# Layer 0 of a two-layer transformer: softmax division traced one step later, block transposes held in place on VectorE, two tails advanced together

## The chip, the core and the metric

The kernel runs on one core of a Trainium2 chip. A core has five engines that run side by side, each through its own list of instructions in order: TensorE (PE, matrix products; PEld is its loading of weights), VectorE (DVE), ScalarE (ACT), GpSimd (POOL) and SyncE (SP, which here only issues DMA transfers). They wait for one another through semaphores. The metric is the time of one execution in microseconds of device time, the median of several runs; lower is better.

## The reference, cut to what matters

The input `x` is 4 sequences of 256 tokens with 512 numbers each, in float32. Two layers follow, each an attention block and a feed-forward block, each with a residual sum and a layer norm after it:

```python
x = L0_attn_x
x = _layernorm(x + _L0_attn_ref(x, ...), axis=-1)
x = _layernorm(x + _L0_ffn_ref(x, ...), axis=-1)
x = _layernorm(x + _L1_attn_ref(x, ...), axis=-1)
x = _layernorm(x + _L1_ffn_ref(x, ...), axis=-1)
```

The change concerns the attention of layer 0: 32 query heads of 16 numbers, 8 key and value heads (each shared by 4 query heads), and a causal mask over 256 tokens:

```python
scores = jnp.einsum('bhqd,bhkd->bhqk', q, k) / jnp.sqrt(jnp.asarray(HEAD_DIM, dtype=jnp.float32))
scores = jnp.where(causal, scores, NEG)
p = jax.nn.softmax(scores, axis=-1)
out = jnp.einsum('bhqk,bhkd->bhqd', p, v)
out = out.transpose(0, 2, 1, 3).reshape(B, S, D_MODEL)
return out @ Wo + bo
```

Its feed-forward block is one product with a 512 x 512 weight, dequantised in the kernel, and a bias. Layer 1's attention has 32 query heads of 128 numbers and a distance bias.

## The kernel before

The kernel is written with a framework that traces instructions in program order, then orders each engine's list by priorities and a plan of its own, and adds the semaphores. Where the code calls `tc.keep_in_program_order(ins)`, the instruction keeps its place in program order on its engine; all others may be moved. Buffers come from pools; a tile with `bufs=n` has n places that are used in turn, and a new tile waits until the old user of its place is done.

**Layer 0's steps.** The work is 64 steps `(b, qt, h, i)`: sequence `b` (4), query tile `qt` of 128 tokens (2), half `h` of the heads (2), and `i` (4). A step handles 4 query heads for 128 queries against 128 keys (`qt` 0) or 256 keys (`qt` 1). It passes through these stages:

- `begin0`: two score products on TensorE (L470) into one of two PSUM tiles `sc`; VectorE adds the causal mask (L475) and takes the negated row maxima `nm` (L478); ScalarE computes four exponentials into `pr` with their row sums `sums` (L274, one instruction and a read of the accumulator each); then `divided`: VectorE's reciprocal of the sums (L279) and GpSimd's multiplication of `pr` by it (L280).
- `transpose0`: the probabilities have to be transposed before the output product. There are two ways. TensorE transposes four 128 x 128 blocks into PSUM (L295) and ScalarE copies them to `prT` (L296, or L102/L100 for the first tiles). Or `transposed_by_blocks`: VectorE transposes 32 x 32 blocks within `pr` (L306), SP stores the result to device memory in four pieces (`way<-blocks`, L312) and loads it back in the right order (`prT<-way`, L316).
- `end0`: after the last `i` of a half, the output products (L515) into `o`; after both halves a copy of `o` to `oT` (L100 on VectorE or L102 on ScalarE in turn), and a tail for this tile of 128 tokens is queued.

`run` drives the steps: at count n it begins step n, calls `fill`, transposes step n - `lag`, and ends step n - `lag` - `more`. Before, both are 3.

**Between the steps.** `fill` advances two queues by one piece each. `ahead` holds `project0(b + 1)`: the transposes of `x` and the key, query and value products of the next sequence (L270, L376, L389, L404). `tails` holds `feed_forward_weight` first and then the tails, `tail0`: output projection (L428), residual sum (L430), layer-norm statistics (L257 to L259), a power on GpSimd (L260), normalisation (L264), transposes of the result `x1` (L270), the addition of the feed-forward bias on GpSimd (L440), the feed-forward product (L444), sum, statistics, power and normalisation again (L448, L257 to L260, L264), and the transposes of the result into `x2T` (L270). A tail is cut into pieces by `yield`; an empty piece (a second `yield` in a row) is a pause. Only the tail at the head of the queue advances.

**The way into layer 1.** The last tails run beside the first products of layer 1: at L717 seven pieces of `project1(0)` alternate with pieces of the tails. Sums over the tokens of `x2T` on GpSimd (`token_sums`, L589 to L592) come after the third. Layer 1 itself (from L682) also uses `divided` and `transposed_by_blocks`, the latter with `room` 2 where layer 0 has 1.

Of the kernel before, what the change touches and what calls it, by code (L numbers as in the profile page):

```python
# [21 lines left out]
B, S, D = 4, 256, 512  # L22
# [37 lines left out]
def block_kernel(  # L60
# [20 lines left out]
    nc = tc.nc  # L81
# [52 lines left out]
    def bank_m(name):  # L134
        return ps_w.tile([P, D], F32, tag="w", name=name)
# [116 lines left out]
    def norm_factors(y, name):  # L252

        st = s0.tile([P, 6], F32, tag="bn", name=f"bn_{name}", bufs=4)
        mv = s0.tile([P, 2], F32, tag="mv", name=f"mv_{name}", bufs=4)
        rs = s0.tile([P, 1], F32, tag="rs", name=f"rs_{name}", bufs=4)
        nc.vector.bn_stats(st, y)  # L257
        nc.vector.bn_aggr(mv, st)
        nc.vector.tensor_scalar(rs, mv[:, 1:2], EPS, 1.0, ALU.add, ALU.mult)  # L259
        powers.append(nc.gpsimd.tensor_tensor(rs, rs, minus_half, ALU.pow))  # L260
        return mv[:, 0:1], rs

    def normalise(dst, y, factors):
        nc.vector.tensor_scalar(dst, y, *factors, ALU.subtract, ALU.mult)  # L264

    def transposed(dst, src, name):

        pt = bank_t(f"pt_{name}")
        for c in range(NC):
            nc.tensor.transpose(pt[:, c, :], src[:, ts(c, P)], ident)  # L270
        evacuate(dst, pt)

    def exponentials(pr, sc, nm, sums, i, w):
        nc.scalar.activation(  # L274
            pr[:, i, 0:w], sc, AF.Exp, bias=nm[:, i : i + 1], accum_out=sums[:, i : i + 1]
        )

    def divided(pr, sums, w):
        nc.vector.reciprocal(sums, sums)  # L279
        nc.gpsimd.tensor_tensor(  # L280
            pr[:, :, 0:w], pr[:, :, 0:w], sums.unsqueeze(2).to_broadcast([P, G, w]), ALU.mult
        )

    def softmax_tiles(sp, name, bufs):
        nm = sp.tile([P, G], F32, tag="nm", name=f"nm_{name}", bufs=bufs + 2)
        sums = sp.tile([P, G], F32, tag="sums", name=f"sums_{name}", bufs=bufs + 2)
        pr = sp.tile([P, G, 2 * P], F32, tag="pr", name=f"pr_{name}", bufs=bufs)
        return nm, sums, pr
# [9 lines left out]
    def transposed_by_blocks(sp, name, pr, nt, dst, room):  # L298

        blocks = sp.tile(
            [P, room, 4, G, 32], F32, tag="blocks", name=f"blocks_{name}", bufs=2 // room
        )
        for kt in range(nt):
            nc.vector.transpose(  # L306
                blocks[:, kt].rearrange("p j h q -> p h j q"),
                pr[:, :, ts(kt, P)].rearrange("p h (j k) -> p h j k", k=32),
            )
        way = dram.tile([2, 4, 32, 4, G * 32], F32, tag="way", name=f"way_{name}")  # L310
        for i in range(4):
            nc.sync.dma_start(  # L312
                way[0:nt, :, :, i, :].rearrange("t j k f -> k (t j) f"),
                blocks[32 * i : 32 * i + 32, 0:nt].rearrange("k t j h q -> k (t j) (h q)"),
            )
        nc.sync.dma_start(  # L316
            dst.rearrange("p t j h q -> p t (j h q)"),
            way[0:nt].rearrange("t j k i f -> (j k) t (i f)"),
        )

    def run(steps, begin, transpose, end, before, fill, lag, more=1, after=None):

        waiting = deque()
        for n in range(len(steps) + lag + more):
            if n < len(steps):
                before(steps[n])
                waiting.append([steps[n], begin(*steps[n])])
            fill()
            if lag <= n < len(steps) + lag:
                item = waiting[min(n - lag, more)]  # L330
                item[1] = transpose(*item[0], item[1])
            if n >= lag + more:
                step, got = waiting.popleft()
                end(*step, got)
            if after:
                after()

    def advance(queue):

        while queue:  # L340
            if next(queue[0], None) is not None:
                return
            queue.popleft()

    def exhaust(queue):
        while queue:
            advance(queue)


    qkv0 = {}  # L350
# [73 lines left out]
    def tail0(tt, oT):  # L424

        py = bank_m(f"py_{tt}")
        for i in range(G):
            nc.tensor.matmul(py, oT[:, i, :], wop[:, i, :], start=(i == 0), stop=(i == G - 1))  # L428
        y = s0.tile([P, D], F32, tag="y", name=f"y_{tt}")
        nc.vector.tensor_tensor(y, py, x[tt], ALU.add)  # L430
        factors = norm_factors(y, f"a{tt}")
        yield True
        x1 = s0.tile([P, D], F32, tag="x1", name=f"x1_{tt}")
        normalise(x1, y, factors)
        yield True
        if tt < NTT - 1:
            yield True
        x1T = s0.tile([P, NC, P], F32, tag="x1T", name=f"x1T_{tt}")
        transposed(x1T, x1, f"x1_{tt}")
        nc.gpsimd.tensor_tensor(x1, x1, fb_b, ALU.add)  # L440
        yield True
        pf = bank_m(f"pf_{tt}")
        for c in range(NC):
            nc.tensor.matmul(  # L444
                pf, x1T[:, c, :], wfT[:, c, :], start=(c == 0), stop=(c == NC - 1)
            )
        y2 = s0.tile([P, D], F32, tag="y", name=f"y2_{tt}")
        nc.vector.tensor_tensor(y2, pf, x1, ALU.add)  # L448
        factors = norm_factors(y2, f"b{tt}")
        yield True  # L450
        x2[tt] = xp.tile([P, D], F32, tag="x", name=f"x2_{tt}")
        normalise(x2[tt], y2, factors)
        yield True
        if tt < NTT - 1:
            yield True
        transposed(x2T[:, :, ts(tt, P)], x2[tt], f"x2_{tt}")
        yield True

    ahead, tails = deque(), deque()

    def begin0(b, qt, h, i):

        qT, kT, _ = qkv0[b]
        w = (qt + 1) * P
        name = f"0_{b}_{qt}_{h}_{i}"
        nm, sums, pr = softmax_tiles(a0, name, 6)
        sc = ps_s0.tile([P, 2, 2, 2 * P], F32, tag="s", name=f"sc_{name}")
        for j in range(2):
            rows = slice(32 * (2 * h + j), 32 * (2 * h + j) + 32)
            nc.tensor.matmul(  # L470
                sc[:, j, :, 0:w], qT[rows, i, ts(qt, P)], kT[rows, :, 0:w], start=True, stop=True
            )
        scf = sc.rearrange("p j e k -> p (j e) k")
        diag = scf[:, :, w - P : w]
        nc.vector.tensor_tensor(  # L475
            diag, diag, causal.unsqueeze(1).to_broadcast([P, G, P]), ALU.add
        )
        nc.vector.tensor_reduce(nm, scf[:, :, 0:w], AX.X, ALU.max, negate=True)  # L478
        for n in range(G):
            exponentials(pr, scf[:, n, 0:w], nm, sums, n, w)  # L480
        divided(pr, sums, w)
        return pr

    open0 = {}
    def transpose0(b, qt, h, i, pr):


        name = f"0_{b}_{qt}_{h}_{i}"
        if i == 0:
            open0["p", h] = a0.tile(  # L490
                [P, 2, G, 4, 4, 32], F32, tag="prT", name=f"prT0_{b}_{qt}_{h}"
            )
        prT = open0["p", h]
        rest = range(qt + 1)
        if (0, 0) < (b, qt) and (b, qt, h) < (B - 1, 1, 1) and (qt == 1 or i % 2 == 0):
            rest = rest[1:]
            transposed_by_blocks(a0, name, pr, 1, prT[:, 0:1, i], 1)
        copy = evacuate if (b, qt) == (0, 0) else nc.scalar.copy
        transposed_probabilities(
            name, pr, [(kt, prT[:, kt, i].rearrange("p j n q -> p n j q")) for kt in rest], copy  # L500
        )
        return prT
# [35 lines left out]
                load_weights1(0)  # L538

    def fill():  # L540
        advance(tails)
        advance(ahead)

    ahead.append(project0(0))
# [6 lines left out]
        before0,  # L551
        fill,
        lag=3,
        more=3,
    )
    la.close()

# [158 lines left out]

    first = project1(0)  # L717
    for n in range(7):
        advance(tails)
        if n == 2:  # L720
            with tc.issue_after(powers[-1].ins):
                token_sums(0, 3 * P)
        next(first)
# [105 lines left out]
    kept = [m1.tile([P, 2, 2, 2 * P], F32, name=f"kept_{b}") for b in range(B)]  # L829
# [199 lines left out]
        for _ in range(due - 1):  # L1029
            advance(ahead)  # L1030

    def after1(newest_first=False):

        for tail in list(tails)[:: -1 if newest_first else 1]:
            if next(tail, None) is None:
                tails.remove(tail)

    run(
        [(kv, b, qt) for kv in range(NKV) for b in range(B) for qt in range(2)],
        begin1,  # L1040
# [2 lines left out]
        before1,  # L1043
        fill1,
        lag=1,
        after=after1,
    )
    while outputs or tails:
        advance(outputs)
        ending.append(True)  # L1050
        after1(True)


# [30 lines left out]
```

## Time and profile before

| | |
|---|---|
| time, median of 3 runs (lowest to highest) | 994.2 us (992.19 to 995.15) |
| the profiled execution's own time | 993.61 us |
| its span | 991.4 us |
| instructions in its profile | 11477 |
| mean granted TensorE clock over the span | 0.975 |
| layer 0 (until the first product of layer 1 starts) | 0 to 303 us |
| layer 1 and the end | 303 to 991.4 us |
| VectorE's block transposes in layer 0 (L306, 25 to 303 us) | 40, of 0.71 us |

One execution was recorded by the hardware profiler. "Busy" is the time in which an engine ran instructions; TensorE's products overlap and their ends are modelled, so a busy TensorE need not be one at its peak. The granted clock is the share of full speed that TensorE was allowed. The view of waits says for which instruction an engine with nothing to do was waiting; the chain of waits follows the work back from the last instruction to whatever released each step. L numbers are lines of the kernel before. Records of a few products are missing from a trace.

### The profile page before, as it was taken

The numbers are of one execution on the slowest core, as the hardware profiler recorded it, in microseconds if no ns is written. First come the engines' busy times: TensorE is split into PE (matmuls) and PEld (weight loads), VectorE is DVE, ScalarE is ACT, GpSimd is POOL, SyncE is SP. The second block draws the span as 40 slices with busy tenths as digits, with TensorE's granted clock in tenths as the row PEclk, the third lists the DMA queues.
The fourth block names the chain that finished last, engine by engine and source line by source line (L and its number), as shares of the span: only waits on it lengthen the run. The fifth ranks groups of instructions, "written<-read, shape, count | busy, mean of one in ns | idle before, by whom it ended". The sixth has DMA issues, their size and how long they took to land.

```text
span 991.4 us, 11477 instructions
## 1 busy us (share of the span) xinstructions
PE 941.6 (95%) x3433; PEld 546.3 (55%) x3433; DVE 620.6 (63%) x1287; ACT 316.3 (32%) x1198; POOL 443.2 (45%) x461
## 2 busy tenths in 40 slices
PE   7989979989989999999999999999999999999996
PEld 5634444443334444566666666666666666667652
DVE  3757766656754345755566666667666666666566
ACT  2545544445451100332312222222222121223442
POOL 2344443443444611443633534543544453467732
PEclk9889999989899999999999999999999999999998
DMA  9325234234322010344443353434353334243001
GB/s 286 127 75 128 67 91 108 63 86 108 75 54 85 21 43 0 75 138 115 123 113 117 113 145 86 145 87 126 97 141 103 107 92 132 76 127 88 1 21 63
DMA packets 105218, 95.42 MB, mean 96 GB/s; under 512 B 9157, under 2 KB 76358, under 8 KB 105158
## 3 DMA queue, kind: packets, MB, share of 16 engines
q1 hardware_dynamic: 104342, 93.26, 33.9%
q10 hardware_dynamic: 816, 1.44, 0.4%
q8 instruction: 27, 0.44, 0.2%
q14 instruction: 33, 0.27, 0.1%
HBM read 60.07 MB, written 34.60 MB: 95 GB/s over the span
## 4 chain that ended last, share of the span: by engine, by line
PE 74%; POOL 11%; DVE 7%; ACT 3%; issue 2%; DMA 2%; SPq 0%; POOLq 0%; DVEq 0%; ACTq 0%
PE p_q L615 18%; PE po L858 14%; PE sc L945 7%; PE o L985 7%; POOL pr L280 5%; PE p_k L615 5%; PE p_v L615 5%; PE o L515 3%; ACT pr L274 3%; PE py L819 3%; PE sc L470 3%; DVE nm L478 2%; PE pt L295 2%; DVE blocks L306 2%; PE pq L389 2%
## 5 line engine op out<-in xcount | busy, mean ns | idle before, releaser
L274 ACT ACTIVATE pr<-sc,nm 128x256 f32<-128x256 f32 (+1 forms) x512 | 208.8, 419 | 408.1 <-DVE nm L961 284.3
L280 POOL TENSOR_TENSOR pr<-pr,sums 128x512 f32<-128x512 f32 (+1 forms) x128 | 188.1, 1470 | 286.6 <-DVE sums L279 270.9
L306 DVE STREAM_TRANSPOSE blocks<-pr 128x512 f32<-128x512 f32 x124 | 85.9, 702 | 76.5 <-POOL pr L280 75.5
L953 DVE SCALAR_TENSOR_TENSOR sc<-table,sc 128x128 f32<-128x128 f32 (+1 forms) x256 | 86.0, 356 | 34.7 <-PE sc L945 32.4
L274 ACT ACTIVATION_READ_ACCUMULATOR pr<-sc,nm 128x1 f32 x512 | 103.7, 203 | 0.0
L945 PEld LDWEIGHTS sc<-kT,qT 128*128 128x128 f32 x512 | 82.3, 191 | 35.2 <-issue 29.2
L945 PE MATMUL sc<-kT,qT 128*128 128x256 f32 (+1 forms) x512 | 95.2, 327 | 0.0
L985 PE MATMUL o<-prT,v 128*128 128x512 f32 x192 | 92.9, 593 | 0.0
L629 DVE TENSOR_TENSOR qT<-p_q,qT 128x512 f32<-128x512 f32 x96 | 64.6, 686 | 35.6 <-PE p_q L615 34.8
L470 PE MATMUL sc<-kT,qT 32*128 32x256 f32 (+1 forms) x256 | 62.8, 568 | 16.7 <-ACT pr L274 16.6
L961 DVE TENSOR_REDUCE nm<-sc 128x2 f32<-128x512 f32 (+1 forms) x128 | 70.2, 551 | 1.5
L478 DVE TENSOR_REDUCE nm<-sc 128x4 f32<-128x512 f32 (+1 forms) x64 | 60.8, 950 | 1.0
L858 PE MATMUL po<-wo,so 128*128 128x256 f32 x224 | 58.0, 381 | 2.1 <-POOL so L595 2.1
L615 PE MATMUL p_q<-x2T,ws_q 128*128 128x512 f32 x128 | 59.8, 592 | 0.0
L615 PE MATMUL p_q<-xt,ws_q 128*128 128x512 f32 x128 | 57.8, 593 | 1.8 <-POOL ws_q L598 1.8
L858 PE MATMUL po<-wo,o 128*128 128x256 f32 x224 | 57.7, 380 | 0.0
L615 PE MATMUL p_q<-x2T,wq 128*128 128x512 f32 x128 | 57.6, 592 | 0.0
L515 PE MATMUL o<-prT,v 128*32 128x512 f32 x192 | 55.8, 670 | 1.0 <-DMA prT<-way 0.7
L102 ACT COPY o<-o 128x512 f32<-128x512 f32 x29 | 17.0, 585 | 124.6 <-PE o L985 124.6
L858 PE MATMUL po<-to,so 128*128 128x256 f32 x224 | 53.3, 381 | 1.0 <-POOL so L598 1.0
L279 DVE RECIPROCAL sums<-sums 128x4 f32<-128x4 f32 x128 | 21.9, 171 | 50.1 <-ACT pr L274 49.8
L858 PEld LDWEIGHTS po<-to,so 128*128 128x128 f32 x224 | 42.2, 190 | 16.3 <-issue 8.8
(156 smaller groups left out, 1430.3 us busy)
## 6 DMA issues: line engine op xcount, KB each, us to landing
way<-blocks SPq DMA_DIRECT2D x272, 64.0 KB, 1.8
prT<-way SPq DMA_DIRECT2D x68, 256.0 KB, 2.7
way<-blocks SPq DMA_DIRECT2D x112, 128.0 KB, 2.5
prT<-way SPq DMA_DIRECT2D x28, 512.0 KB, 3.7
wq<-in_L_attn_w_qkv_dram SPq DMA_DIRECT2D x8, 1024.0 KB, 5.1
wo<-in_L_attn_w_o_dram SPq DMA_DIRECT2D x8, 1024.0 KB, 5.1
wk<-in_L_attn_w_qkv_dram SPq DMA_DIRECT2D x4, 512.0 KB, 3.7
wv<-in_L_attn_w_qkv_dram SPq DMA_DIRECT2D x2, 1024.0 KB, 6.2
```

The lines of the kernel that those rows point to most:

```text
L274: nc.scalar.activation(pr[:, i, 0:w], sc, AF.Exp, bias=nm[:, i : i + 1], accum_out=sums[:, i : i + 1])
L280: nc.gpsimd.tensor_tensor(pr[:, :, 0:w], pr[:, :, 0:w], sums.unsqueeze(2).to_broadcast([P, G, w]), ALU.mult)
L306: nc.vector.transpose(blocks[:, kt].rearrange("p j h q -> p h j q"), pr[:, :, ts(kt, P)].rearrange("p h (j k) -> p h j k", k=32),)
L470: nc.tensor.matmul(sc[:, j, :, 0:w], qT[rows, i, ts(qt, P)], kT[rows, :, 0:w], start=True, stop=True)
L478: nc.vector.tensor_reduce(nm, scf[:, :, 0:w], AX.X, ALU.max, negate=True)
L515: nc.tensor.matmul(o[32 * r : 32 * r + 32, :], v[:, kt, r, ts(e, 32)], prT[:, kt, :, :, 2 * j + e, :], start=(kt == 0 and e == 0), stop=(k ...
L615: nc.tensor.matmul(bank, fixed, moving, start=(c == 0), stop=(c == 1))
L858: nc.tensor.matmul(bank[:, ts(n, HALF)], left[:, c, :], right[:, c, :], start=(c == 0), stop=(c == 1),)
L945: nc.tensor.matmul(sc[:, m, 0:w], qT[:, 2 * j + m, b * S + qt * P : b * S + (qt + 1) * P], kT[:, b * S : b * S + w], start=True, stop=True,)
L953: nc.vector.scalar_tensor_tensor(sc[:, m, 0:w], table[:, 2 * P - w :], slopes[kv * G + 2 * j + m], sc[:, m, 0:w], ALU.mult, ALU.add,)
L961: nc.vector.tensor_reduce(nm[:, 2 * j : 2 * j + 2], sc[:, :, 0:w], AX.X, ALU.max, negate=True)
L985: nc.tensor.matmul(o, v1[:, 2 * b + kt, ts(kv, P)], prT[:, kt].rearrange("p j h q -> p h j q"), start=(kt == 0), stop=(kt == qt),)
```

## The change

It has five parts, all in layer 0.

- The division of a step is no longer traced in its own `begin0`. The step's `pr` and `sums` go into `undivided`, and `divide0` divides them in the next step's `begin0`, after that step's exponentials are traced (or in `rest` when there is no next step). The reciprocal keeps its place in program order.
- The block transposes of layer 0 (`room` 1) keep their place in program order on VectorE.
- For `qt` 1 the first three of four `i` go through block transposes where all four did; the fourth goes through TensorE. For `qt` 0 it stays with `i` 0 and 2.
- `fill` advances every tail in the queue by one piece (`advance_all`) where it advanced the first one; two pauses are added to each tail but the last. In layer 1 `advance_all` takes the place of `after1`, which did the same.
- `more` goes from 3 to 2: a step ends, and the output products are traced, one step earlier.

```diff
-    def divided(pr, sums, w):
-        nc.vector.reciprocal(sums, sums)
+    def divided(pr, sums, w, kept=False):
+        ins = nc.vector.reciprocal(sums, sums)
+        if kept:
+            tc.keep_in_program_order(ins)
         nc.gpsimd.tensor_tensor(
...
-            nc.vector.transpose(
+            ins = nc.vector.transpose(
                 blocks[:, kt].rearrange("p j h q -> p h j q"),
                 pr[:, :, ts(kt, P)].rearrange("p h (j k) -> p h j k", k=32),
             )
+            if room == 1:
+                tc.keep_in_program_order(ins)
...
-    def run(steps, begin, transpose, end, before, fill, lag, more=1, after=None):
+    def run(steps, begin, transpose, end, before, fill, lag, more=1, after=None, rest=None):
...
                 waiting.append([steps[n], begin(*steps[n])])
+            elif rest:
+                rest()
             fill()
...
+    def advance_all(queue, newest_first=False):
+
+        for work in list(queue)[:: -1 if newest_first else 1]:
+            if next(work, None) is None:
+                queue.remove(work)
...
         if tt < NTT - 1:
             yield True
+            yield True
         x1T = s0.tile([P, NC, P], F32, tag="x1T", name=f"x1T_{tt}")
...
         if tt < NTT - 1:
+            yield True
             yield True
         transposed(x2T[:, :, ts(tt, P)], x2[tt], f"x2_{tt}")
...
-        divided(pr, sums, w)
+        divide0()
+        undivided.append((pr, sums, w))
         return pr
 
     open0 = {}
+    undivided = []
+
+    def divide0():
+
+
+        if undivided:
+            divided(*undivided.pop(), True)
+
...
-        if (0, 0) < (b, qt) and (b, qt, h) < (B - 1, 1, 1) and (qt == 1 or i % 2 == 0):
+        if (0, 0) < (b, qt) and (b, qt, h) < (B - 1, 1, 1) and i in ((0, 2), (0, 1, 2))[qt]:
             rest = rest[1:]
             transposed_by_blocks(a0, name, pr, 1, prT[:, 0:1, i], 1)
...
     def fill():
-        advance(tails)
+        advance_all(tails)
         advance(ahead)
...
         lag=3,
-        more=3,
+        more=2,
+        rest=divide0,
     )
...
     for n in range(7):
-        advance(tails)
+        advance_all(tails)
```

More of the change, by code (lines that the diff above doesn't have):

```diff
@@ L1030, in fill1 @@
             advance(ahead)
[L1032 to L1036, printed above, removed]
     run(
@@ L1045, in block_kernel @@
         lag=1,
-        after=after1,
+        after=lambda: advance_all(tails),
     )
@@ L1050, in block_kernel @@
         ending.append(True)
-        after1(True)
+        advance_all(tails, True)
 _INS = [
```

## The prediction

> **What bounds the kernel now.** I read the page first, then the stretches of time, then who waited for whom, then one piece of the chain of waits. On the page (rows 1 and 2) TensorE is busy 95% of the span, but the second row shows where it is not: its digits fall below 9, and the granted clock below full, in the first 13 of 40 slices, which is layer 0 (slice 40 is the end of the program).
>
> ```profile
> PE 941.6 (95%) x3433; PEld 546.3 (55%) x3433; DVE 620.6 (63%) x1287; ACT 316.3 (32%) x1198; POOL 443.2 (45%) x461
> ...
> PE   7989979989989999999999999999999999999996
> ...
> PEclk9889999989899999999999999999999999999998
> ```
>
> The table of stretches (length, busy us of PE, PEld, DVE, ACT, POOL, then granted clock and DMA share) splits layer 0 by sequence:
>
> ```profile
> 76.00:151.00 75.00, 67.18 (x292) 34.66 (x292) 52.89 (x103) 38.63 (x154) 34.32 (x29) 0.94 0.38 98
> 151.00:226.00 75.00, 67.64 (x278) 32.16 (x277) 49.01 (x94) 35.58 (x144) 31.92 (x26) 0.91 0.35 86
> 25.00:303.00 278.00, 250.12 (x1040) 120.21 (x1039) 181.59 (x343) 140.17 (x557) 118.11 (x93) 0.92 0.34 87
> ```
>
> From 25 to 303 us TensorE idles 278.0 - 250.1 = 27.9 us, and its clock averages 0.92, which is 0.08 x 278 = 22 us of full-speed time not granted. No other engine is near full (DVE 65%, ACT 50%, POOL 42%, DMA 34%), so the stalls are waits. The waits in the same stretch (total us, times, longest):
>
> ```profile
> PE sc L470 <- ACT pr L274: 16.6, 12, 3.8
> PE pt_x L270 <- DVE x L264: 4.7, 3, 1.7
> ```
> ```profile
> ACT pr L274 <- DVE nm L478: 70.2, 31, 6.2
> ```
> ```profile
> DVE blocks L306 <- POOL pr L280: 30.0, 24, 2.1
> DVE sums L279 <- ACT pr L274: 21.0, 19, 3.7
> ```
>
> TensorE waits for a score bank that ScalarE's exponentials still hold, ScalarE waits for VectorE's maxima, and VectorE stands 51 us, with later maxima queued behind it, for a block transpose whose probabilities GpSimd has not divided, or for sums not yet added up. The chain of waits (start, us, what) has it in one piece:
>
> ```profile
> 49.59 1.90 POOL pr L280
> ...
> 51.52 0.71 DVE blocks L306
> ...
> 52.46 1.90 POOL pr L280
> ...
> 54.39 0.71 DVE blocks L306
> 55.10 0.60 DVE sc L475
> ...
> 59.05 2.08 PE sc L470 x4
> ```
>
> Two divisions, each followed by its own block transpose, put the mask at 55.1; TensorE idles from 56.0 to 59.05.
>
> [...]32.34 to 35.75 us eight matmuls of L376 take 3.41 us where the same eight take 1.92 later, and the clock is 0.50 in 30-35 us and in 205-210 us, each after a stall. [...]
>
> **The change, part by part.** Its order of instructions on each engine, beside that of before, gives the counts.
>
> *Division a step later.* Of the 63 reciprocals of layer 0 that have a next step, before has 25 ahead of the next mask, 14 between mask and maxima, 24 after the maxima; now all 63 come after. The wait of a reciprocal for ScalarE (21.0 us) therefore stands behind maxima already handed over. Eight exponentials take 1.94 us (row of 47.21 us in the chain), mask and maxima 0.68 + 1.22 = 1.90 us, so little wait is left. Queued behind it now: block transposes and copies, and GpSimd's multiply (1.90 us), which has idle time.
>
> *Block transposes pinned.* Before, 20 of 40 follow their own reciprocal with no mask or maxima between; now 31 of 33 come two or three maxima after it, some 8 us, against 1.90 us of multiply. The 30.0 us wait goes from VectorE. Late next is the tail: an output product, its sum, statistics, a power on GpSimd, the normalisation, all ahead of a mask. At 121-130 us this holds the maxima for 8.7 us and TensorE for 3.8; I expect about 1.3 of the 3.8 to stay, since only one 0.71 us transpose and some of the waiting leave that piece.
>
> *Seven transposes to TensorE.* Block transposes fall from 40 to 33: 7 x 0.71 = 5.0 us off VectorE, and 35 DMA issues off SP (28 stores, 7 loads). Neither is on the path: VectorE will have slack and DMA is at 34%. TensorE gets 7 x 4 transposes. Four take 0.60 to 0.66 us in the trace; with a weight load and the switch ahead of them 0.76 more in the worst rows. I take 0.9 each: **+6.3 us**, bounds 7 x 0.6 = 4.2 and 7 x 1.42 = 10. All of it lies on the path, TensorE being the bound. ScalarE gets 7 copies of 0.60 us = 4.2, covered by its 50% idle time; without that cover they would delay exponentials by the same 4.2 us.
>
> *Tails two at once, a pause longer.* No instruction more. On GpSimd's queue a tail's power (0.55 us) now goes ahead of a multiply (1.90 us) that it used to follow, in most tails of sequences 1 to 3. The transposes of x1 and x2 stand later in TensorE's order, after the power and normalisation they wait for (the 4.7 us row, and 1.5 us of L295 behind the same). At the end of layer 0 the x2 transposes of tile 6 move past the first key product (3.43 us); the sums over tokens on GpSimd, which began at 306.71 behind a power, then start about 1.2 us later, covered by the output product before 317. I add **+0.5**, bounds 0 to 3.
>
> *One step less before the output product.* Nothing added or removed; see the slower rival.
>
> *Gain in stalls:* 75% of 16.6 = 12.5; of 4.7 + 1.5, 80% = 5; of 2.2 us of transposes waiting for a division, 0.7 (the last at 284 us stays). Sum **-18**. *Gain in clock:* 22 us were lost; [...]I take half of it, rounded down: **-10**. Bounds on both: only 8 and 3, if the tails set the maxima; 24 and 20, if hardly a stall is left.
>
> Layer 1's instructions and their order are unchanged; it only starts earlier. Sum: -18 - 10 + 6.3 + 0.5 = -21.2. The profiled execution took 993.6 (span 991.4 and 2.2 around it), 0.6 below the median of 994.2; taken off it gives 972.4, and I centre on the median: **973**. The mechanism's ends are 994 - 44 + 4 = 954 and 994 - 11 + 10 = 993.
>
> **The rivals.** *The clock stays low (983).* [...]For it: at 146.6-149.5 two gaps of 0.7 and 1.5 us were enough for 0.52 afterwards. Against: 100-125 us has gaps of 0.4 to 1.8 and a clock of 1.00. Then -18 + 6.8 = -11.
>
> *The change does little of what it says (990).* The order already had 24 reciprocals behind the maxima, and VectorE's next wait (8.4 us for output products at L100, 8.1 for scores at L475) takes the place of the removed ones. Then -8 - 3 + 6.8 = -4.
>
> *Slower: the transposed blocks come too late (1011).* Their way through memory is 0.71 us of transpose, four stores of 0.43 us to issue, 1.8 us to land, a load of 2.8 us: about 7 us. On SP a load is queued behind the first stores of the next block, which wait for that block's pinned transpose. Before, 4 to 5 steps lay between the last transpose of a half and the product at L515; now about 3, some 12 us, so 5 us are left at the tightest place. If steps shorten to 2.3 us, or the queue adds 5, the product waits. Behind it wait the copy of `o`, and in three places VectorE's maxima, which now stand after that copy. At 2 us in each of 14 halves, and no clock gained: -21 + 28 + 10 = +17. Against it: only 1.7 us of waiting for these loads before, and fewer DMAs.
>
> **How the numbers follow.** A measurement of this kernel tells about 0.3% (3 us) from no change. The main case has 0.62, the low clock 0.16, the small effect 0.10, the slow case 0.12. The first two are faster by over 3 us, and half of the small effect: 0.83; the other half, 0.05, is no change; 0.12 slower. The range of 957 to 993 leaves out the slow case and the far ends of the main one.
>
> **What would show it.** Right: the waits of L306 for GpSimd and of L279 for ScalarE fall from 51 to under 12 us; TensorE's wait for the exponentials under 6; the start of layer 1's first product (303 us) near 282; granted clock over layer 0 about 0.96. The added transposes show as 251 instead of 223 instructions of L295 in that stretch. Wrong: L515 waiting for its load over 5 us in all, VectorE's copy of `o` growing well past 8.4 us with maxima behind it, or the first product of layer 1 after 300.

## The result, and the profile after

The changed kernel takes **982.4 us** (median; 981.7 to 983.7), the kernel before 993.2 (four executions; the table above has three of them). The ratio is 0.989, 95% interval 0.987 to 0.991: about 11 us faster, half of the 21 forecast, inside the range of 957 to 993.

The page of the changed kernel (span 981.8 us; the busy row, then 40 slices of the span):

```profile
PE 936.3 (95%) x3461; PEld 546.8 (56%) x3461; DVE 615.1 (63%) x1280; ACT 320.7 (33%) x1205; POOL 444.8 (45%) x461
...
PE   7999999979889999999999999999999999999996
...
PEclk9999999997899999999999999999999999999999
```

The first nine slices now have a clock of 9 tenths or more; before, it fell to 8 in slices 2, 3, 9 and 11. But TensorE is busy 7, 9, 8 and 8 tenths in slices 9 to 12, with a clock of 7 and 8 tenths in slices 10 and 11: that is sequence 3 (202 to 271 us) and the end of layer 0; a slice is 24.5 us. The table of stretches, cut at the first maxima of sequences 1, 2 and 3, at the last maxima and at layer 1's first product (columns as in the prediction, the last column GB/s), of the changed kernel and then of the kernel before:

```profile
25.00:69.19 44.19, 42.00 (x226) 25.31 (x224) 37.93 (x72) 29.08 (x114) 24.37 (x18) 1.00 0.34 107
69.19:134.62 65.43, 61.70 (x280) 31.57 (x280) 47.88 (x90) 36.88 (x148) 31.42 (x26) 1.00 0.32 81
134.62:202.23 67.61, 63.70 (x280) 31.79 (x280) 47.88 (x91) 36.85 (x147) 31.38 (x26) 0.97 0.32 79
202.23:271.39 69.16, 59.24 (x208) 23.49 (x208) 40.49 (x77) 34.09 (x140) 26.01 (x22) 0.83 0.29 72
271.39:293.09 21.70, 17.91 (x76) 7.75 (x77) 4.35 (x9) 7.17 (x21) 6.63 (x5) 1.00 0.05 16
```
```profile
25.00:81.44 56.44, 49.30 (x221) 29.22 (x221) 39.70 (x74) 29.35 (x115) 25.37 (x19) 0.85 0.34 104
81.44:152.42 70.98, 64.01 (x276) 31.88 (x273) 48.89 (x93) 35.15 (x143) 31.23 (x26) 0.96 0.37 94
152.42:226.71 74.29, 66.93 (x275) 31.96 (x273) 48.30 (x92) 35.58 (x146) 31.05 (x25) 0.91 0.34 86
226.71:284.22 57.51, 52.87 (x206) 20.11 (x203) 40.35 (x79) 34.84 (x144) 25.35 (x21) 0.93 0.38 93
284.22:302.95 18.73, 16.96 (x70) 6.97 (x69) 4.36 (x8) 5.25 (x15) 5.11 (x4) 1.00 0.00 1
```

So by the start of sequence 3 the change has won 12.25 + 5.55 + 6.68 = **24.5 us**, more than the forecast for the whole; sequence 3 and the end then **give back 14.6**. TensorE's busy column splits both: up to sequence 3 it idles 21.5 us before and 9.8 after, and is busy 12.8 us less with no product fewer, so at a higher clock (0.99 against 0.91 over this part); from there on it idles 7.3 us more and is busy 7.3 us more, at a lower one (0.87 against 0.95). Layer 1 takes 688.7 us (688.5 before).

The waits from 25 to 293 us (total, times, longest), TensorE's and VectorE's:

```profile
PE sc L484 <- ACT pr L274: 8.1, 6, 3.3
PE pt L297 <- POOL pr L282: 7.2, 5, 2.0
PE o L538 <- DMA prT<-way: 3.3, 2, 1.8
...
DVE sc L489 <- PE sc L484: 26.5, 18, 3.6
DVE y L442 <- PE py L440: 16.2, 7, 6.9
DVE y L461 <- PE pf L457: 15.8, 7, 8.9
DVE oT L100 <- PE o L538: 15.4, 5, 4.9
DVE sums L279 <- ACT pr L274: 6.1, 6, 2.4
```

The 51 us that VectorE stood for sums and multiplies have become 6.1. It now waits for TensorE's products instead, once for 6.9 us, and its idle time as a whole has only gone from 96.4 (278.0 - 181.6) to 89.6 us (268.1 - 178.5). On TensorE the wait for exponentials has halved (16.6 before), and the wait for probabilities that GpSimd has not yet divided has grown from 2.2 to 7.2. The timeline of TensorE and VectorE shows the place of the 6.9 us (start, us; in brackets the idle time before it and what ended it):

```profile
255.48 1.13 PE L484 MATMUL sc<-kT,qT 32*128 32x512 f32 x4 [1.92 <-ACT pr L274]
...
257.79 2.07 PE L484 MATMUL sc<-kT,qT 32*128 32x512 f32 x2 [1.18 <-ACT pr L274]
...
259.79 5.78 PE L440 MATMUL py<-wop,oT 128*128 128x512 f32 x8
...
265.61 0.69 DVE L442 TENSOR_TENSOR y<-py,x 128x512 f32<-128x512 f32 x1 [6.91 <-PE py L440]
```

Two score products meet with nothing between them, and each waits for the exponentials. The clock drops (0.50 from 259 to 262 us). The second product is cut in two by the scheduler, and its other half (at 265.94) stands behind an output projection that takes 5.78 us at the low clock (3.70 at 225 us, at a clock of 1.00). VectorE stands for the projection's result, whose sum is ahead of the mask in its queue: 11.7 us pass without new maxima.

### The profile page after: what moved, and what is told of

It reads as the page before. It is cut to its first block, busy times and chain, and to the rows that moved or that the text cites. A ratio compares the mean times of both kernels' runs of the same rounds, so it can differ in the third digit from the quotient of the medians.

```text
span 981.8 us, 11455 instructions
## 1 busy us (share of the span) xinstructions
PE 936.3 (95%) x3461; PEld 546.8 (56%) x3461; DVE 615.1 (63%) x1280; ACT 320.7 (33%) x1205; POOL 444.8 (45%) x461
## 4 chain that ended last, share of the span: by engine, by line
PE 82%; POOL 7%; DVE 5%; ACT 2%; DMA 1%; issue 1%; SPq 0%; POOLq 0%; DVEq 0%; ACTq 0%
PE p_q L639 18%; PE po L882 14%; PE sc L969 8%; PE o L1009 8%; PE p_k L639 5%; PE p_v L639 5%; PE o L538 5%; PE sc L484 4%; PE pf L457 3%; PE py L440 3%; PE py L843 3%; PE pq L401 3%; PE pt L297 2%; POOL pr L282 2%; ACT pr L274 2%
## 5 line engine op out<-in xcount | busy, mean ns | idle before, releaser
L308 DVE STREAM_TRANSPOSE blocks<-pr 128x512 f32<-128x512 f32 x117 | 80.5, 697 | 45.8 <-POOL pr L282 45.5
L484 PE MATMUL sc<-kT,qT 32*128 32x256 f32 (+1 forms) x256 | 66.1, 561 | 8.3 <-ACT pr L274 8.1
L985 DVE TENSOR_REDUCE nm<-sc 128x2 f32<-128x512 f32 (+1 forms) x128 | 70.1, 550 | 1.5
L489 DVE TENSOR_TENSOR sc<-sc,causal 128x512 f32<-128x512 f32 x64 | 43.9, 686 | 29.2 <-PE sc L484 29.0
L297 PE MATMUL pt<-ident,pr 128*128 128x128 f32 x300 | 45.3, 279 | 11.3 <-POOL pr L282 9.2
L297 PEld LDWEIGHTS pt<-ident,pr 128*128 128x128 f32 x300 | 34.2, 141 | 34.5 <-issue 16.8
```

Of the source, the lines that this page charges most:

```text
L297: nc.tensor.transpose(pt[:, i, :], pr[:, i, ts(kt, P)], ident)
L308: ins = nc.vector.transpose(blocks[:, kt].rearrange("p j h q -> p h j q"), pr[:, :, ts(kt, P)].rearrange("p h (j k) -> p h j k", k=32),)
L484: nc.tensor.matmul(sc[:, j, :, 0:w], qT[rows, i, ts(qt, P)], kT[rows, :, 0:w], start=True, stop=True)
L985: nc.vector.tensor_reduce(nm[:, 2 * j : 2 * j + 2], sc[:, :, 0:w], AX.X, ALU.max, negate=True)
```

## The experiments

Each kernel is one of the two with a change that is shown further down. The stretches are those above, from the profiled run (sequence 0 from 25 us on); "end" is the last one. The ratio is to the kernel before on the same chip. A row of stretches is one execution, and the executions of one kernel can differ by several us (u_seven 993.8 to 1005.0, d_div_pin 993.6 to 1001.5), so a difference of 2 or 3 us in one stretch is not shown to repeat.

| kernel | us | ratio [95%] | seq. 0 | seq. 1 | seq. 2 | seq. 3 | end |
|---|---|---|---|---|---|---|---|
| before | 993.2 | 1 | 56.4 | 71.0 | 74.3 | 57.5 | 18.7 |
| after | 982.4 | 0.989 [0.987, 0.991] | 44.2 | 65.4 | 67.6 | 69.2 | 21.7 |
| u_div | 996.1 | 1.004 [1.002, 1.006] | 50.9 | 69.6 | 65.2 | 70.1 | 24.6 |
| u_pin | 985.1 | 0.991 [0.989, 0.994] | 48.7 | 68.7 | 68.3 | 59.9 | 21.0 |
| u_seven | 997.6 | 1.006 [1.004, 1.007] | 43.6 | 73.9 | 73.1 | 65.1 | 23.0 |
| u_tails | 981.1 | 0.989 [0.985, 0.992] | 43.9 | 67.4 | 68.0 | 67.3 | 18.6 |
| u_i123 | 994.5 | 1.001 [1.000, 1.002] | 43.6 | 72.5 | 74.1 | 67.3 | 21.2 |
| u_seven_o | 1003.5 | 1.010 [1.009, 1.012] | 43.9 | 75.7 | 73.0 | 73.7 | 21.2 |
| u_more | 979.7 | 0.987 [0.984, 0.990] | 42.9 | 75.4 | 69.0 | 54.8 | 20.9 |
| c_pin3 | 980.5 | 0.988 [0.985, 0.990] | 43.2 | 67.1 | 66.0 | 67.3 | 21.0 |
| c_mix | 981.0 | 0.987 [0.986, 0.989] | 43.7 | 65.5 | 67.5 | 66.2 | 20.9 |
| d_div_pin | 998.9 | 1.004 [1.002, 1.007] | 43.7 | 76.4 | 72.6 | 67.6 | 23.1 |
| d_seven | 986.7 | 0.994 [0.992, 0.995] | 56.8 | 69.3 | 70.7 | 55.8 | 18.7 |
| d_div_pin_seven | **974.8** | **0.980 [0.978, 0.982]** | 43.6 | 69.5 | 65.4 | 58.6 | 22.3 |

### One part undone at a time

My theory was that the 24.5 us came from VectorE's freed queue (later division, kept block transposes); the rival, that they came from the tails.

*u_div*, the division in its own step:

```diff
-        divide0()
-        undivided.append((pr, sums, w))
+        divided(pr, sums, w)
```

> The changed kernel with one part undone: each division is traced in its own step again and may be placed freely. Freed-queue theory (the 24.5 us won up to sequence 3 come from VectorE no longer waiting between two maxima for sums and multiplies): VectorE waits for sums again, 10 to 20 us in layer 0 against 6.1; the start of sequence 3 moves from 202 back to 208 to 214, the time is 988 to 994. Tails theory (the tails two at once with longer pauses made the 24.5 us): the start of sequence 3 stays within 2 us of 202, the time within 3 us of 982.4. Theory on the last part (the 14.6 us given back in sequence 3 come from score products, output products and their copies in a fixed order with no projections between them, whatever the division does): sequence 3 and the end of layer 0 still take about 91 us.

Measured: 996.1 us. VectorE waits 32.0 us for sums again (6.1 in the changed kernel; 10 to 20 were expected), sequence 3 starts at 210.7, and sequence 3 and the end take 94.7 us. The freed-queue theory holds for the division: the loss is even over the 988 to 994 expected, and lies in sequences 0 and 1 (6.7 and 4.2 us; sequence 2 is 2.4 us shorter). Sequence 3 is no shorter without the later division.

*u_pin*, the block transposes free:

```diff
-            if room == 1:
-                tc.keep_in_program_order(ins)
```

> The changed kernel with the block transposes free to be placed by the scheduler again. Freed-queue theory: the block transposes move up beside their multiply, VectorE waits 10 to 30 us for GpSimd again (none in the changed kernel), the start of sequence 3 moves from 202 to 208 to 216, the time is 987 to 996. Tails theory: start of sequence 3 within 2 us of 202, time within 3 us of 982.4. If blocks that stand late are what costs the 14.6 us in sequence 3 (the slower rival of the forecast), sequence 3 and the end get shorter by 5 us or more here; by the theory of fixed order without projections they stay at about 91 us.

Measured: 985.1 us; the intervals of this kernel and of the changed one overlap. The trace behaves as the theory has it and the time does not: VectorE waits 33.0 us for GpSimd again and sequence 3 starts 8.5 us later, at 210.7, but sequence 3 and the end take 80.9 us in place of 90.9. 33 us of waiting on VectorE came back, cost 8.5 us up to sequence 3, and a sequence 3 and end shorter by 10.0 us made up for it (in the profiled execution, the fastest of six; their median is 2.7 us above the changed kernel's). The shorter sequence 3 is what late blocks would explain; c_pin3 below tests that.

*u_seven*, all four `i` of a second query tile by blocks. (This concerns its first 128 keys; the probabilities of its other 128 keys go through TensorE in every kernel here.)

```diff
-        if (0, 0) < (b, qt) and (b, qt, h) < (B - 1, 1, 1) and i in ((0, 2), (0, 1, 2))[qt]:
+        if (0, 0) < (b, qt) and (b, qt, h) < (B - 1, 1, 1) and (qt == 1 or i % 2 == 0):
```

> The changed kernel with all four transposes of a second query tile by blocks again (40 block transposes in place of 33, 28 TensorE transposes fewer). The forecast charged the seven 6.3 us, all on TensorE's path: then 976 here. If VectorE's 0.71 us each and the way through memory matter instead (the output product waits for a block), 984 to 990 with a wait of the output product for its load above 5 us (3.3 in the changed kernel). If both balance, within 3 us of 982.4.

Measured: 997.6 us, slower than each of the three expectations, and without the wait of the output product for its load that one of them had. Sequences 1 and 2 lose 8.5 and 5.5 us and are back at about the level of the kernel before. The timeline of TensorE at that place:

```profile
85.14 0.70 PE L484 MATMUL sc<-kT,qT 32*128 32x256 f32 x4
85.77 0.66 PE L297 MATMUL pt<-ident,pr 128*128 128x128 f32 x4
86.44 0.70 PE L484 MATMUL sc<-kT,qT 32*128 32x256 f32 x4
90.29 0.70 PE L484 MATMUL sc<-kT,qT 32*128 32x256 f32 x4 [3.15 <-ACT pr L274]
91.69 1.22 PE L484 MATMUL sc<-kT,qT 32*128 32x256 f32 x4 [0.70 <-ACT pr L274]
```

Four score products nearly in a row; the third waits 3.15 us for exponentials to free its bank. In the changed kernel the second half of the output product (3.63 us) runs from 86.23, between the two parts of the second of them, and the output projection follows. The same gap of 3.15 us stands at 161.5. At that point the orders differ: with the last group's probabilities transposed on TensorE, the scheduler places the output product two score products earlier.

*u_tails*, tails one after the other, with one pause less ahead of `x1T` and of `x2T` (the first edit also in layer 1's first seven advances):

```diff
-        advance_all(tails)
+        advance(tails)
...
         if tt < NTT - 1:
-            yield True
             yield True
```

> The changed kernel with the tails one after the other again and the shorter pauses. Tails theory: the start of sequence 3 moves from 202 to 215 or later, TensorE's wait for x from below 1 to above 4 us, the time 993 or more. Freed-queue theory: the start of sequence 3 stays at 202 to 206; sequence 3 and the end of layer 0 take 91 us as before if the tails have no share in what was given back, 80 to 86 us if two tails at once hold up VectorE there; time 975 to 987.

Measured: 981.1 us, no difference from 982.4. Sequence 3 starts at 204.3, so the tails theory falls, though the wait for x that it named is back: TensorE waits 4.4 us for x again. Its wait for divisions is 1.5 us in place of 7.2, which makes up for it. Sequence 3 and the end take 85.9 us, at the upper edge of the 80 to 86 expected if two tails at once have a share in what was given back: 5 us, 3 of them in the end.

### What the seven transposes do

*u_i123*: the same number of transposes on TensorE, but of the first group of heads and not of the last.

```diff
-        if (0, 0) < (b, qt) and (b, qt, h) < (B - 1, 1, 1) and i in ((0, 2), (0, 1, 2))[qt]:
+        if (0, 0) < (b, qt) and (b, qt, h) < (B - 1, 1, 1) and i in ((0, 2), (1, 2, 3))[qt]:
```

> The changed kernel, second query tiles: the transpose that goes to TensorE is that of the first group of four heads (i = 0) in place of the last (i = 3); as many block transposes, TensorE transposes and DMAs as in the changed kernel. Theory of place (undoing the seven cost 15 us because the transposes of the last group stood between the last score products and the output product, and kept TensorE busy there): sequences 1 and 2 take 70 to 74 us each as with the seven undone, not 65.4 and 67.6, and the time is 990 to 998. Theory of load (VectorE's 0.71 us for each block transpose less, or four transposes of filling for TensorE wherever they stand): within 3 us of 982.4.

Measured: 994.5 us, sequences 1 and 2 at 72.5 and 74.1, gaps of 3.12 and 3.11 us back at 87.65 and 161.51. It is the place, not VectorE's load nor TensorE's filling as such: the last group's transposes gain, the first group's do not.

*u_seven_o*: all by blocks, and the output product put ahead of the second score product traced after it (`o_end` is the last product of the half, `o_n` the step after which it was traced; the loop issues the score products).

```diff
+        held = open0["o_end"] if open0["n"] == open0.get("o_n", -9) + 2 else None
+        with tc.issue_after(held) if held else ExitStack():
+            for j in range(2):
```

> The changed kernel with all transposes of a second query tile by blocks again, and one order written out by hand: the second score product traced after an output product stands behind it on TensorE, which puts the output product between two score products where the changed kernel has it. Theory of filling (the seven gained because they let the output product stand between two score products that otherwise meet while the exponentials still hold the bank): the 3.1 us waits near 87 and 161 us are gone, sequences 1 and 2 take 64 to 69 us each, the time is 978 to 986. Theory that the transposes themselves are wanted there (the transposed blocks of the last group come too late through memory): the output product waits for its load by 1.5 us or more in most of the halves, sequences 1 and 2 stay at 71 to 74 us, the time at 992 to 1000.

Measured: 1003.5 us, above both expectations. The filling theory's claim that the order alone does it is refuted; the order was had, and the wait moved: score products wait 5.7 us for exponentials (15.9 in u_seven), output products 9.3 us for their loads. TensorE's waits from 25 to 293 us, then the queue of SyncE, then TensorE's timeline:

```profile
PE pt L297 <- POOL pr L282: 13.8, 8, 2.7
PE o L541 <- DMA prT<-way: 9.3, 4, 3.8
```
```profile
85.10 3.63 SPq L316 DMA_DIRECT2D way<-blocks  x4
88.89 0.34 SPq L320 DMA_DIRECT2D prT<-way  x1
```
```profile
87.17 0.70 PE L487 MATMUL sc<-kT,qT 32*128 32x256 f32 x4 [0.22 <-ACT pr L274]
91.69 4.76 PE L541 MATMUL o<-prT,v 128*32 128x512 f32 x12 [3.83 <-DMA prT<-way]
```

The block transpose of the last group starts at 86.72, its last store is issued by 88.73, its load is issued at 88.89 and the product that needs it starts at 91.69: 5.0 us, against 86.23 for the output product in the changed kernel. Either the product stands late and score products wait for exponentials (u_seven), or it stands early and waits for memory. With the last group on TensorE neither happens at this place. The load is late in four of the halves, not in most as the second theory had it, and the waits for divisions grow as well (13.8 us against 7.2), so memory is not all of the 21 us.

### Which parts make the gain

*d_div_pin*, the kernel before with only the later division and the kept block transposes (in the diff of the change, these two alone):

> The kernel before with only the division a step later and the block transposes kept in place (all second query tiles by blocks, tails one after the other, short pauses, the long distance to the output product). If these two are enough for the gain: 980 to 986, VectorE's waits for sums and multiplies below 10 us. If the seven transposes on TensorE are needed beside them (their undoing alone cost 15 us): 990 to 1000, with those waits below 10 us all the same and TensorE waiting 12 us or more for the exponentials.

Measured: 998.9 us, **slower than before** (1.002 to 1.007). Its waits from 25 to 303 us, VectorE's and TensorE's:

```profile
DVE sc L487 <- PE sc L482: 29.1, 18, 7.2
...
DVE sums L279 <- ACT pr L274: 5.5, 9, 2.0
```
```profile
PE pt L297 <- POOL pr L282: 13.2, 5, 3.3
PE sc L482 <- ACT pr L274: 10.8, 9, 2.9
```

VectorE's 51 us of waiting are 5.5, as in the changed kernel. Sequence 0 wins its 12.7 us; sequence 1 loses 5.4, sequence 3 10.1 and the end 4.4 (the profiled execution, 999.5, is one of the slower ones). TensorE's wait for exponentials was put at 12 or more and is 10.8; the longest in total is now that for divisions, 13.2 (2.2 before). In sequence 1 the score products meet as in u_seven, and again at 165.5:

```profile
90.98 0.70 PE L482 MATMUL sc<-kT,qT 32*128 32x256 f32 x4
91.61 0.33 PE L270 MATMUL pt_x<-ident,x 128*128 128x128 f32 x1
94.80 0.70 PE L482 MATMUL sc<-kT,qT 32*128 32x256 f32 x4 [2.86 <-ACT pr L274]
```

*d_seven*, the kernel before with only the seven transposes:

> The kernel before with the seven transposes on TensorE alone; division, block transposes, tails and the distance to the output product as before. If they gain by themselves: 981 to 988, with VectorE's waits for sums and multiplies still at 40 us or more. If they need the later division beside them (its undoing cost 14 us with the seven in place): 990 to 1000. By the forecast's own sum, 6.3 us of transposes on the path and nothing won, 1000.

Measured: 986.7 us (0.992 to 0.995), with VectorE's waits still 24.7 + 19.8 = 44.5 us. They gain 6.4 us by themselves, in sequences 1 to 3.

*d_div_pin_seven*, these three parts together, without the tails and with the long distance to the output product (`more=3`):

> The kernel before with three parts of the change: the division a step later, the block transposes kept in place, and the seven transposes on TensorE; tails one after the other, short pauses and the long distance to the output product as before. In its order on TensorE no two score products of sequence 1 or 3 stand next to each other, and none of sequence 3 is cut around an output projection. Theory that the seven are what makes the later division pay (without them the same kernel took 998.9): 966 to 975, sequences 1 and 2 at 66 to 69 us each, sequence 3 at 55 to 59, first product of layer 1 at 277 to 284. If the tails two at once and the shorter distance carry a share of what the change gained: 983 to 988.

Measured: **974.8 us**, ratio 0.978 to 0.982, the fastest of all and 9 us below the changed kernel by the ratios. From 25 us to layer 1's first product the four corners take 278.0 us (none), 283.4 (division and pinning), 271.3 (the seven) and 259.4 (all three): +5.4 and -6.7 alone, -18.5 together. So the later division and the kept transposes pay only beside the seven. At the place just shown, TensorE now has the output product ahead of the next score product, and none waits:

```profile
88.41 0.70 PE L482 MATMUL sc<-kT,qT 32*128 32x256 f32 x4
89.04 0.55 PE L270 MATMUL pt_x<-ident,x 128*128 128x128 f32 x3
89.52 3.63 PE L536 MATMUL o<-prT,v 128*32 128x512 f32 x16
```

Over layer 0 TensorE waits 2.7 us for exponentials (10.8) and 8.8 for divisions (13.2). The timeline of TensorE in sequence 3 answers to that of the changed kernel at 255 us:

```profile
252.13 1.13 PE L482 MATMUL sc<-kT,qT 32*128 32x512 f32 x4
253.19 1.98 PE L440 MATMUL py<-wop,oT 128*128 128x512 f32 x4
255.11 1.13 PE L482 MATMUL sc<-kT,qT 32*128 32x512 f32 x4
256.16 1.98 PE L440 MATMUL py<-wop,oT 128*128 128x512 f32 x4
```

Half a projection stands on each side of a score product, nothing waits, and both halves together take 3.96 us at the full clock (1.00 from 245 to 265 us). Sequence 3 takes 58.6 us, as before the change.

### What was given back in sequence 3

*u_more*, the old distance (`more=3`):

> The changed kernel with the step before the output product given back (four steps from a step's maxima to its output product plus three more, as before the change). The order on TensorE no longer cuts the third to last score product of sequence 3 in two around the output projection. Theory that this cut is the 11.7 us without new maxima at 257 to 269 us: that gap falls to 5 us or less and the time to 973 to 978. Theory that the gap comes from the half-rate clock after TensorE's waits of 1.9 and 1.2 us just ahead of it: the gap stays above 8 us, the time within 4 us of 982.4.

Measured: 979.7 us. Sequence 3 takes 54.8 us; the longest stretch without maxima in its last part is 7.0 us (260.07 to 267.10), between the two expectations. But sequence 1 takes 75.4, so most of it is lost elsewhere.

*c_mix*, the old distance in sequence 3 only (`more` is 2 for b < 3, then 3):

> The changed kernel with the output product one step earlier in sequences 0 to 2 only; in sequence 3 it stands at the old distance. With the old distance everywhere sequence 3 took 54.8 us in place of 69.2, but sequence 1 75.4 in place of 65.4. If both belong to their own sequences: start of sequence 3 at 200 to 204, sequence 3 at 54 to 59, first product of layer 1 at 276 to 282, time 966 to 972. If sequence 3 was short there only because its start came 10 us later: sequence 3 at 65 or more, time 976 to 983.

Measured: 981.0 us, sequence 3 at 66.2. The second expectation holds: the distance, changed in sequence 3 alone, does not shorten it. A wait of 3.29 us at 214 us, where score products of sequence 3 meet, stands here as in the changed kernel.

*c_pin3*, block transposes free in sequence 3 only:

```diff
-            if room == 1:
+            if room == 1 and "_3_" != name[1:4]:
```

> The changed kernel with the block transposes kept in place in sequences 0 to 2 only, free in sequence 3. With all of them free sequence 3 up to the last maxima took 59.9 us in place of 69.2, but the part up to sequence 3 8.5 us more. If both effects belong to their own sequences: start of sequence 3 at 202 to 204, sequence 3 at 60 to 63 us, time 973 to 977. [...]sequence 3 stays at 66 to 70 us, time within 4 us of 982.4.

Measured: 980.5 us, sequence 3 at 67.3, within the 66 to 70 of the second expectation, so blocks that stand late in sequence 3 do not by themselves cause its length. Its stall of 3.22 us at 213.5 is the same.

With the other three parts in place, tails and distance give four kernels:

| sequence 3 (sequences 0 to 2) | short distance | long distance |
|---|---|---|
| tails two at once | 69.2 (177.2), the change | 54.8 (187.3), u_more |
| tails one at a time | 67.3 (179.3), u_tails | 58.6 (178.5), d_div_pin_seven |

Among these four the distance sets sequence 3, and the tails matter little there. In sequences 0 to 2 the long distance costs 10 us beside two tails at once and nothing beside one at a time. That fits what the times say: undoing both gains 9 us, undoing either gains little.

It is no rule for sequence 3 by itself: u_pin has the short distance and takes 59.9 there, d_div_pin has the long one and takes 67.6. What goes with the length in all fourteen kernels is the clock granted in sequence 3: 0.93 to 0.97 where it takes 54.8 to 59.9 us, 0.78 to 0.87 where it takes 65.1 to 73.7. Which order of instructions keeps that clock is open. Why the long distance, and free block transposes (u_pin), shorten sequence 3 when changed for all sequences and not when changed for the last one alone (c_mix, c_pin3) is open too; a late start is not the reason, for d_div_pin_seven starts sequence 3 at 203.5.

## Why the prediction was right and wrong

**Right: what bounds the kernel, and the marks on VectorE.** The waits for sums and multiplies fell from 51 to 6.1 us (forecast: under 12). The clock went from 0.92 to 0.95 (forecast 0.96): 0.05 x 268 = 13 us not granted, against 22, so 9 won of 10 forecast (half of the 22, the author's estimate). 252 transposes are recorded, 251 were expected. Layer 1 takes the same time.

**Failed: "Gain in stalls", -18.** TensorE's idle time fell only by 4.4 us, from 27.9 to 268.1 - 244.6 = 23.5. This is the term that the sum had wrong: with 9 won of clock and 4.3 spent on the added transposes it gives -9, and layer 0 is 9.9 us shorter. By its parts: the wait for exponentials fell by 8.5 us to 8.1 (forecast 12.5, to under 6), the waits behind the tails by 6.2 (forecast 5); the wait for divisions, which was to fall by 0.7, rose by 5.0, the output products' wait for loads by 2.6, others by about 3. The wait for divisions is 1.7 us with the later division undone (u_div); the tails undone bring it to 1.5 as well (u_tails), but d_div_pin_seven, without them, has 8.8. Layer 1's first product is at 293 (forecast 282).

The step that failed is the inference from a wait gone on VectorE to a stall gone on TensorE. It holds in sequence 0, where the later division and the kept transposes win 12.7 us by themselves. In d_div_pin the waits on VectorE are gone, yet TensorE idles longer than before (29.4 us), for score products that meet and for divisions.

**Failed: "Seven transposes to TensorE", +6.3, "neither is on the path".** A transpose takes 38.5 / 252 = 0.153 us of TensorE, so 28 take 4.3, near the lower bound of 4.2. But the block path that they leave was on the path: the last group's 5.0 us through memory bear on where the output product can stand without a wait (u_seven, u_seven_o). The term is not +6.3 but -6.4 alone, and about -15 inside the change (997.6 less 982.4; the profiled spans differ by 11). The slower rival had this very mechanism, transposed blocks too late. In the changed kernel the output products wait 3.3 us for loads, so it did not decide; that the seven transposes take away its place is what u_seven_o suggests, where the wait is 9.3 us, 3.83 of it at the tightest place. The prediction weighed both and did not join them.

**Failed: "Tails two at once", +0.5, and "One step less", nothing.** Each undone alone moves the time by 1 to 3 us, within the intervals. Both undone together win 9 us: 10.6 in sequence 3, less a little elsewhere. Sequence 3 has no projections of a next sequence to fill TensorE; that this is why the loss falls there is likely, and not shown. The prediction argued with averages over layer 0 and did not look at the last sequence by itself.

**The rivals.** "The clock stays low" gave 983, the number measured, but the clock was low in sequence 3 alone: 0.99 up to it and 0.83 in it. (Against this rival the prediction set gaps of 0.4 to 1.8 us at 100 to 125 us; the trace has only two there, of 0.45 and 0.47.) "Little of what it says" is excluded by the 24.5 us won by the start of sequence 3. One sign of being wrong did come: VectorE's wait to copy `o` grew from 8.4 to 15.4 us, with maxima right behind it at 89.91 and 155.69. The forecast's own bounds also reach further than it says, to 994 - 11 + 10 + 3 = 996, since the 993 leaves out the tails' 3. So the sign and the range were right, but the agreement within 10 us was in part luck, for the terms were wrong in both directions: the seven transposes, which gain by themselves, were booked as a cost, and the tails with the shorter distance, which lose 9 us, as nothing.

## What to carry to other kernels

When a wait is taken off a helper engine, look at the bounding engine's order next: what stands between two products that share a bank, and which operand keeps the filler from standing there. The last of a group of operands sets when the product that consumes all of them can run; here it paid to route that one by the shorter path (6.4 us in d_seven), although it costs time on the busiest engine (0.153 us a transpose). And read gains by stage: one stage can give back what the others win.

## What the runs showed of the hardware

The clock was lost after short waits. In sequence 3 of the changed kernel TensorE waits 1.68 us once (231.35 to 233.03), and the clock is 0.50 from 235 to 241 us though TensorE is busy without a break:

```profile
232.00:235.00 3.00, 1.97 (x8) 1.01 (x8) 2.50 (x7) 2.10 (x11) 1.56 (x3) 0.71 0.25 56
235.00:238.00 3.00, 3.00 (x12) 1.22 (x8) 2.01 (x4) 1.20 (x8) 1.88 (x2) 0.50 0.51 107
238.00:241.00 3.00, 3.00 (x7) 1.04 (x4) 2.89 (x5) 1.93 (x8) 1.37 (x2) 0.50 0.32 102
```

In the kernel before, two waits of 0.41 and 0.73 us between 75.7 and 77.5 us were followed by 0.56 over the next 3 us. But a wait of 1.57 us at 103.6 in the changed kernel left the clock at 1.00, and so did two waits of 1.96 and 1.60 us that end at 272.56 and 275.68. So the length of a wait does not decide alone: 0.73 us was followed by a clock of 0.56, 1.96 us by 1.00. What else decides is not shown.
